# Four-layer graph network: the last 106 attention targets by gathered edge slots instead of in the dense units

## The chip, the cores and the metric

The kernel runs on one core of a Trainium2 chip. The metric is the device time of one execution in microseconds (us). One core has five engines that run their own instruction queues: TensorE (PE; its weight loads are listed as PEld), VectorE (DVE), ScalarE (ACT), GpSimd (POOL) and SyncE (SP). In this kernel SP issues nearly all plain transfers, and POOL issues the indirect ones (gathers).

## The reference

A graph with N = 6250 nodes and E = 206250 directed edges (sorted by target; each node has an edge to itself) passes through four layers. Each one adds its result to x and normalises the row. D = 128, four attention heads of 32 columns.

```python
x = ln(x + L0(x))    # mean over neighbours, two linear maps
x = ln(x + L1(x))    # per edge: relu([x[src], edge_attr] @ W1 + b1) @ W2, mean over a target's edges, then an MLP
x = ln(x + L2(x))    # per target: sum of x[src] and edge_attr through linear maps, then a small MLP
x = ln(x + L3(x))    # graph attention:
    h = (x @ W).reshape(N, 4, 32)
    a_src, a_dst = sum(h * att_src), sum(h * att_dst)          # per node and head
    logits = leaky_relu(a_src[src] + a_dst[dst], 0.2)           # per edge; the kernel's self edge is apart
    alpha = softmax of logits over the edges of a target
    out = segment_sum(h[src] * alpha, dst)
    out = relu(ln(out + bias) * gamma + beta)
```

## The kernel before

The nodes are 49 blocks of 128 (the last has 106). They are tiled as `groups` of four blocks (twelve full groups and one of 106 rows) and as `duos` of two. The fast path, `fast()`, runs four stages one after the other. The order within a stage is written out by hand: generators (`yield` between steps) are advanced a step at a time between the matmuls, and every engine takes its instructions in program order.

**First adjacency product (`dense0`, up to about 840 us).** For each pair of blocks `search` and `find` locate a target's edges by gathers, `sort` holds 64 edge slots per target and marks which are its own (`mine`), and a dense count matrix `A` is built from one-hots by PE and stored in DRAM as `adj` (one row of 256 targets for each pair). The same stage multiplies it with x for layer 0. The lists of all edges (`src_i`, and `dst_r` relative to a chunk's first target `w0b`) are loaded as a whole.

**Edge MLP (`mlp`, to about 3392 us).** The edges run in 147 chunks of 128 x 11. Each chunk is three loads of four or fewer columns; `load` runs five such units ahead and gathers rows of `t1` by `src_i`. `onehot(c)` makes on VectorE the matrix that sums a chunk's edges into a window of 64 targets.

**Second adjacency product (`dense2`).** For each pair of blocks, `load(sb)` brings five tiles of `adj` by SP (four of 704 KB with six buffers, and a smaller one), and 147 matmuls follow. `node2` for the pair before is advanced between them, a step after every ten matmuls; its last step computes the attention logits `al` with VectorE (L523, L525).

**Attention (`attend`).** For a head h and a target's logit, the exponential of the leaky relu is one of two products of a source factor and a target factor, chosen by a comparison. So the sums over all sources are dense matmuls with `adj`. `tables` prepares the source side for a head (h times `us`, split into three bfloat16 parts: ScalarE casts, POOL subtracts the part, L1198). Then for each unit, two groups of targets, 1024 in all, a loop runs over 25 pairs of source blocks. In each step SP loads `A` three steps ahead; ScalarE makes `r` (L1320, two rows), VectorE makes `B` (L1327) and `C` (L1329), PE does five products for each group into `s` (L1347). Six units cover the twelve full groups. The 106 remaining targets are the `more` of the last unit: they have their own load `Am`, their own two VectorE operations `Bm` (L1333, L1334) and five matmuls `sm` (L1349). In the text units are counted from 1 to 6.

Between the steps three lanes are advanced, each by one step every second time: `sums` (`close` of the last unit: copies of s, products with `fold`, division; and `targets` for the next unit), `news` (`tables` for the next head) and `ends` (`finish3`, the final normalisations of a group, started in head 3 and drained after the last matmul).

Of the kernel before, what the change touches and what calls it, by code (L numbers as in the profile page):

```python
# [9 lines left out]
F32 = mybir.dt.float32  # L10
BF16 = mybir.dt.bfloat16
I32 = mybir.dt.int32
# [56 lines left out]
def kernel(  # L69
# [38 lines left out]
    dram = ctx.enter_context(tc.tile_pool(name="dram", bufs=1, space=bass.MemoryType.DRAM))  # L108
    setup = ctx.enter_context(ExitStack())
# [8 lines left out]
    t3 = dram.tile([N, HW], F32)  # L118
    t3d = dram.tile([N + W, 2 * HEADS], F32)
# [24 lines left out]
    src_i = const.tile([P, NCH, T], I32)  # L144
    dst_r = const.tile([P, NCH, T], F32)
# [128 lines left out]

    def prepare_chunks(prep, pps):

        dst_i = dst_r.bitcast(I32)
        nc.vector.memset(src_i[:, NCH - 1, :], 0)
        nc.vector.memset(dst_i[:, NCH - 1, :], -1)
        for to, of in ((dst_i, dst), (src_i, src)):  # L280
            if NF:
                nc.sync.dma_start(to[:, :NF, :], of[: NF * P * T].rearrange("(c p t) -> p c t", p=P, t=T))
            if tail:
                nc.sync.dma_start(to[:tail, NF, :], of[NF * P * T :].rearrange("(p t) -> p t", t=T))
# [25 lines left out]
        nc.vector.tensor_sub(dst_r, dst_r, w0b.unsqueeze(2).to_broadcast([P, NCH, T]))  # L310
# [183 lines left out]
    def node2(acc, al, pool, pps, n0, rows, nb, G=4, hT=None):  # L494
# [32 lines left out]
        if not keep:  # L527
            nc.vector.tensor_copy(hs[:rows, :nb, D:], al[:rows, 0, b0 : b0 + nb, :])
            store(t3, hs, n0, rows, nb)
# [103 lines left out]
    def general():  # L633
        with ExitStack() as st:
            gp = st.enter_context(tc.tile_pool(name="gacc", bufs=1))
            acc = gp.tile([P, 3, NA], F32, name="gacc")
            for k in range(3):
# [4 lines left out]
                           allow_small_or_imprecise_dtypes=True)  # L642
            row_i = gp.tile([P, NCH], I32, name="row_i")
# [3 lines left out]
            def edges(name, rows_of):  # L647
                with tc.tile_pool(name=f"{name}s", bufs=1) as ep, \
# [5 lines left out]
                    nc.vector.tensor_copy(node, dst_r[:, ds(c, 1), :].rearrange("p c t -> p (c t)"))  # L654
                    w0 = ep.tile([P, 1], F32, name="w0")
                    nc.vector.tensor_copy(w0, w0b[:, ds(c, 1)])
                    ri = ep.tile([P, 1], I32, name="ri")
                    nc.vector.tensor_copy(ri, row_i[:, ds(c, 1)])
                    nc.vector.tensor_scalar(node, node, w0, None, op0=ALU.add)
# [96 lines left out]
    def fast():  # L756
# [24 lines left out]

        def onehot(ep, c, bufs=2):
            K = sizes[c]
            oh = ep.tile([P, T, W], F32, name="oh", bufs=bufs)
            nc.vector.tensor_tensor(
                oh[:K], iota[:K, :W].unsqueeze(1).to_broadcast([K, T, W]),
                dst_r[:K, c, :].unsqueeze(2).to_broadcast([K, T, W]), ALU.is_equal)
# [12 lines left out]
        def dense0(stack):  # L800
# [21 lines left out]
            with tc.tile_pool(name="d0o", bufs=1) as one, tc.tile_pool(name="d0", bufs=1) as ep, \  # L822
# [39 lines left out]
                def sort(sb):  # L862
# [5 lines left out]
                    nc.vector.tensor_reduce(degc[:, 2 * sb : 2 * sb + 2], mine, AX.X, ALU.add)  # L868
# [548 lines left out]
```

## Time and profile before

| | |
|---|---|
| Time, median of 5 runs | 5435.55 us (5431.06 to 5441.93) |
| The profiled execution | 5444.59 us, its span 5442.8 us |
| PE busy | 4956.3 us, 91% of the span |
| VectorE, ScalarE, POOL busy | 3008.6, 2594.2, 1989.8 us |
| Mean granted TensorE clock | 0.944 |
| Chain that ended last, by engine | PE 41%, ACT 7%, DVE 5% |

The profile lists groups of instructions by line (L1347 is line 1347 of the kernel before), engine and operation, with `out<-in` by the program's names, the number of instructions, their busy time and the mean of one in ns, then the idle time ahead of them and what ended it. The view in order of time gives start, length and instruction, and in brackets the idle time before it. "SPq" is a transfer being issued by SP. A PE matmul's end is modelled, so busy PE time isn't the same as PE at its peak; a matmul of f32 data shows as two records.

### The profile page before, as it was taken

How to read it: one execution, taken by the hardware profiler on the slowest of the kernel's cores; microseconds unless marked ns; L12 is line 12 of the kernel's file. 1: busy time of each engine (PE TensorE's matmuls, PEld its weight loads, DVE VectorE, ACT ScalarE, POOL GpSimd, SP SyncE). 2: the span in 40 equal slices, each digit the busy share in tenths (PEclk: the TensorE clock that was granted, in tenths of full speed). 3: DMA queues.
4: the chain of work that ended last, by engine and by line, in shares of the span. 5: the costliest groups of instructions: out<-in, count | busy, mean ns of one | idle time of the engine just before them, and what ended most of it. 6: DMA issues, size and time to landing. Idle time of an engine off the chain costs nothing.

```text
span 5442.8 us, 90752 instructions
## 1 busy us (share of the span) xinstructions
PE 4956.3 (91%) x33855; PEld 4079.6 (75%) x33855; DVE 3008.6 (55%) x5084; ACT 2594.2 (48%) x3617; POOL 1989.8 (37%) x1966
## 2 busy tenths in 40 slices
PE   4999998899998998999998998999699999999995
PEld 3999997888888888888888888899455555555553
DVE  6888873233333333333332333222588888888998
ACT  3444442233332333333332332100599999999984
POOL 3334325666666566666666665000110010010000
PEclk9999998898998989999998998999899999999997
DMA  6333334444444444444444443555377777777773
GB/s 120 123 125 141 129 123 134 125 124 128 129 128 124 122 126 128 125 132 126 128 128 125 124 130 117 175 190 190 114 216 219 221 216 228 213 214 228 213 212 118
DMA packets 599589, 834.35 MB, mean 153 GB/s; under 512 B 119837, under 2 KB 484313, under 8 KB 594917
## 3 DMA queue, kind: packets, MB, share of 16 engines
q1 hardware_dynamic: 513077, 603.59, 36.0%
q0 software_dynamic: 85072, 224.21, 14.0%
q8 instruction: 272, 4.46, 0.3%
q14 instruction: 176, 1.44, 0.1%
q10 hardware_dynamic: 992, 0.66, 0.0%
HBM read 738.23 MB, written 89.88 MB: 152 GB/s over the span
## 4 chain that ended last, share of the span: by engine, by line
PE 41%; ACT 7%; DVE 5%; issue 2%; DMA 1%; another core or an unknown queue 1%; POOL 1%; SPq 0%; DVEq 0%; ACTq 0%; POOLq 0%
PE s L1347 13%; PE seg L1107 9%; PE sum L798 7%; PE pre L1093 6%; ACT r L1320 6%; DVE B L1327 2%; PE tp L1082 2%; PE na L1239 1%; DMA A<-adj 1%; PE na L448 0%; SPq L1283 0%; PE sm L1349 0%; DVE sT L1232 0%; ACT acc L1196 0%
## 5 line engine op out<-in xcount | busy, mean ns | idle before, releaser
L127 POOL DMA_INDIRECT g<-t,src_i x1617 | 1571.0, 972 | 962.3 <-issue 756.8
L1320 ACT ACTIVATE r<-ad,bias 128x1024 bf16<-128x1024 f32 (+1 forms) x1176 | 1276.6, 1154 | 90.9 <-DVE B L1327 57.0
L1095 DVE TENSOR_TENSOR g<-g,pre 128x512 f32<-128x512 f32 x882 | 548.7, 640 | 1272.9 <-PE pre L1093 374.0
L1347 PEld LDWEIGHTS <-acc 128*99 128x99 bf16 x5856 | 697.4, 126 | 604.5 <-issue 155.2
L1107 PE MATMUL seg<-oh,g 128*128 128x64 f32 (+1 forms) x6468 | 1026.9, 282 | 51.9 <-issue 47.8
L1107 PEld LDWEIGHTS seg<-oh,g 128*128 128x128 f32 (+1 forms) x6468 | 949.0, 203 | 94.7 <-issue 62.6
L1093 PE MATMUL pre<-W1s,eaT 128*128 128x256 f32 (+1 forms) x3234 | 883.4, 415 | 106.8 <-issue 50.0
L1347 PE MATMUL s<-B,acc 128*99 128x512 bf16 x3504 | 884.2, 382 | 89.5 <-DVE B L1327 84.0
L1096 ACT ACTIVATE g<-g 128x512 f32<-128x512 f32 x882 | 506.7, 592 | 677.6 <-DVE g L1095 440.9
L1093 PEld LDWEIGHTS pre<-W1s,eaT 128*128 128x128 f32 (+1 forms) x3234 | 632.5, 208 | 222.5 <-issue 101.9
L1327 DVE TENSOR_TENSOR B<-A,r 128x2048 bf16<-128x2048 bf16 x600 | 722.8, 1205 | 118.9 <-ACT r L1320 91.8
L1084 ACT COPY eaT<-tp 128x512 f32<-128x512 f32 (+1 forms) x441 | 240.8, 546 | 1055.8 <-remote 312.9
L1107 PE MATMUL seg<-oh,ea 128*128 128x64 f32 (+1 forms) x3234 | 659.1, 285 | 34.0 <-issue 33.2
L1107 PEld LDWEIGHTS seg<-oh,ea 128*128 128x128 f32 (+1 forms) x3234 | 522.6, 202 | 33.7 <-issue 33.3
L907 ACT CAST A<-pa 128x784 bf16<-128x784 f32 x400 | 324.4, 811 | 350.0 <-PE pa L904 322.1
L798 PE MATMUL sum<-A,xs 128*128 128x256 bf16 (+1 forms) x3675 | 469.4, 274 | 0.4 <-ACT A L907 0.4
L1198 POOL TENSOR_TENSOR xs<-xs,acc 128x264 f32<-128x264 f32 (+1 forms) x104 | 103.6, 1004 | 992.9 <-ACT acc L1196 971.4
L1329 DVE TENSOR_TENSOR C<-A,B 128x1024 bf16<-128x1024 bf16 x600 | 430.3, 717 | 63.6 <-PE s L1347 0.8
L798 PE MATMUL sum<-A,acc 128*128 128x256 bf16 (+1 forms) x3675 | 409.3, 271 | 3.3 <-DMA A<-adj 3.3
L798 PEld LDWEIGHTS <-acc 128*128 128x128 bf16 x3675 | 355.1, 98 | 44.8 <-issue 4.8
L798 PEld LDWEIGHTS <-xs 128*128 128x128 bf16 x3675 | 358.4, 102 | 36.2 <-issue 0.6
L904 PE MATMUL pa<-oh,oh 128*128 128x98 bf16 x3200 | 355.9, 269 | 27.6 <-ACT A L907 23.0
(229 smaller groups left out, 4475.6 us busy)
## 6 DMA issues: line engine op xcount, KB each, us to landing
A<-adj SPq DMA_DIRECT2D x2304, 128.0 KB
ea<-in_edge_attr_dram SPq DMA_DIRECT2D x292, 256.0 KB
A<-adj SPq DMA_DIRECT2D x100, 704.0 KB
ea<-in_edge_attr_dram SPq DMA_DIRECT2D x146, 192.0 KB
g<-t,src_i POOLq DMA_INDIRECT x1617
Am<-adj SPq DMA_DIRECT2D x96, 128.0 KB
A<-adj SPq DMA_DIRECT2D x25, 320.0 KB
t<-y SPq DMA_DIRECT2D x24, 256.0 KB
```

Of the source, the lines that this page charges most:

```text
L127: nc.gpsimd.indirect_dma_start(out=to, out_offset=None, in_=table, in_offset=bass.IndirectOffsetOnAxis(ap=index[:K, t : t + 1], axis=0))
L798: nc.tensor.matmul(ps[:, :n], parts[part][:, b, :], a(b)[:, :n], start=k == 0, stop=k == 3 * NB - 1)
L904: nc.tensor.matmul(ps[:, o, q * LO : (q + 1) * LO], ohs[g][0][:, 2 * j + o, :, q], ohs[g][1][:, 2 * j + o, :, q], start=True, stop=True)
L907: nc.scalar.copy(A[sb][:, :, q0 : q0 + 2 * QI].rearrange("p k (o q) -> p k o q", q=QI), ps[:, :, : QI * LO].rearrange("p o (q k) -> p k o ...
L1093: nc.tensor.matmul(pre[:K, t, :], eaT[i][:, b + t, :K], W1s[:, 1, :], start=True, stop=True)
L1095: nc.vector.tensor_add(gb, gb, pre[:K, :n, :])
L1096: nc.scalar.activation(gb, gb, AF.Relu)
L1107: nc.tensor.matmul(ps[:, m, :], rows, oh[c][:K, a + t, :], start=a + t == 0 and m == 0, stop=a + t == T - 1, skip_group_check=True)
L1320: nc.scalar.activation(r[:, l, : n + m], ad[:, : n + m], AF.Relu, bias=bias[:, b + l, h : h + 1], scale=BIG)
L1327: nc.vector.tensor_tensor(wide(bt), At[:, :ns, :kk, :w], wide(r), ALU.min)
L1329: nc.vector.tensor_sub(ct[:, :n].rearrange("p (s q) -> p s q", q=w), At[:, :ns, 0, :w], bt[:, 0, :n].rearrange("p (s q) -> p s q", q=w))
L1347: nc.tensor.matmul(s[to][g][:M, : c1 - c0], row, rhs(c0, c1), start=to not in begun, stop=stop)
```

## The change

The dense units now cover the twelve full groups alone. The 106 targets of the last block are computed from their edge slots: `sort` stores for them the sources (`slot_src`, zero where a slot isn't theirs) and a mask (`slot_not`) in DRAM; `node2` stores h and the source logit of every node in `t3`, a row of 132 numbers; in `attend` a fourth lane, `others`, advances `gathered` every third step. It gathers eight slots at a time, 64 in all, forms the exponentials with VectorE and ScalarE, multiplies and sums with the identity as the stationary operand; the target's own edge comes in as a first matmul. The division and `finish3` follow at once.

To make room in SBUF, the whole edge lists go: `mlp` loads the edges of a chunk from DRAM, six chunks ahead, and `onehot` subtracts `w0b` itself. In `tables`, VectorE subtracts in place of POOL. The tile `s` of `attend` shares the buffer of `neg`.

```diff
@@ storage
+    UNITS = max(1, (len(groups) - 1) // 2)
+    rest = groups[2 * UNITS :]
+    R0 = rest[0][0] // P if rest else NB
+    slot_src = dram.tile([max(2, 2 * NS - R0 // 2 * 2), P, S], I32)
+    slot_not = dram.tile([max(2, 2 * NS - R0 // 2 * 2), P, S], F32)
-    src_i = const.tile([P, NCH, T], I32)
-    dst_r = const.tile([P, NCH, T], F32)
@@ node2
-        if not keep:
+        if keep:
+            for c, of in ((slice(0, D), hs), (slice(D, HW), al[:, 0, b0 : b0 + nb, :])):
+                nc.sync.dma_start(t3[n0 : n0 + n, c].rearrange("(b p) d -> p b d", p=rows), of[:rows, :nb])
+        else:
@@ fast: edges of a chunk
+        def load_edges(c):
+            if c < NCH:
+                edges[c] = edge_pool.tile([P, 2, T], I32, name="edges", bufs=8)
+                for k, of in enumerate((src, dst)):
+                    nc.sync.dma_start(edges[c][: sizes[c], k, :],
+                                      of[c * P * T : c * P * T + sizes[c] * T].rearrange("(p t) -> p t", t=T))
         def onehot(ep, c, bufs=2):
             K = sizes[c]
+            at = ep.tile([P, T], F32, name="at", bufs=2)
+            nc.vector.tensor_scalar(at[:K], edges.pop(c)[:K, 1, :], w0b[:K, c : c + 1], None, op0=ALU.subtract)
...
-                dst_r[:K, c, :].unsqueeze(2).to_broadcast([K, T, W]), ALU.is_equal)
+                at[:K].unsqueeze(2).to_broadcast([K, T, W]), ALU.is_equal)
@@ dense0, sort
+                    if 2 * sb + 2 > R0:
+                        k0 = 2 * sb - R0 // 2 * 2
+                        of = ep.tile([P, 2, S], I32, name="of")
+                        nc.vector.tensor_tensor(of, s, mine, ALU.mult)
+                        nc.sync.dma_start(slot_src[k0 : k0 + 2].rearrange("b p s -> p b s"), of)
+                        none = ep.tile([P, 2, S], F32, name="none")
+                        nc.vector.tensor_scalar(none, mine, -1.0, 1.0, op0=ALU.mult, op1=ALU.add)
+                        nc.sync.dma_start(slot_not[k0 : k0 + 2].rearrange("b p s -> p b s"), none)
@@ dense0, third step
                             flush_dma(nc.sync)
+                            for c in range(6):
+                                load_edges(c)
@@ mlp, load
+                    if a == 0:
+                        load_edges(c + 6)
                     for t in range(k):
-                        gather(g[i][:K, t, :], t1, src_i[:, c, :], a + t, K)
+                        gather(g[i][:K, t, :], t1, edges[c][:, 0, :], a + t, K)
@@ attend
-            units = [(g[0][0], g, []) for g in (groups[k : k + 2] for k in range(0, len(groups), 2))]
-            if len(units) > 1 and len(units[-1][1]) == 1 and units[-1][1][0][2] == 1:
-                units[-2][2].extend(units.pop()[1])
+            units = [(groups[2 * k][0], groups[2 * k : 2 * k + 2]) for k in range(UNITS)]
...
-                s = one.tile([P, NB, HEADS], F32, name="s")
+                s = one.tile([P, NB, HEADS], F32, name="neg")
...
+                shift = one.tile([P, max(1, NB - R0), HEADS], F32, name="shift")
+                es = one.tile([P, max(1, NB - R0), HEADS], F32, name="es")
+                if rest:
+                    nc.vector.scalar_tensor_tensor(shift, s[:, R0:], SLOPE, s[:, R0:], op0=ALU.mult, op1=ALU.max)
+                    nc.vector.tensor_add(es, al[:, 0, R0:], al[:, 1, R0:])
+                    nc.vector.scalar_tensor_tensor(es, es, SLOPE, es, op0=ALU.mult, op1=ALU.max)
+                    nc.vector.tensor_sub(es, es, shift)
+                    nc.scalar.activation(es, es, AF.Exp)
@@ attend, tables
-                                nc.gpsimd.tensor_sub(xs[:, :nb], xs[:, :nb], tab[:, bs, :, k, :])
+                                nc.vector.tensor_sub(xs[:, :nb], xs[:, :nb], tab[:, bs, :, k, :])
@@ attend, the new lane
+                def gathered():
+                    Q = 8
+                    chunks = [(g, j, q) for g, (n0, rows, nb) in enumerate(rest) for j in range(nb) for q in range(0, S, Q)]
+                    def issue(i):
...
+                            rows_of[i] = ep.tile([P, Q, HW], F32, name="g3", bufs=4)
+                            for t in range(Q):
+                                gather(rows_of[i][:, t, :], t3, slots[g, j][0], q + t, P)
+                    for i in range(3):
+                        issue(i)
+                    yield 8
+                    for i, (g, j, q) in enumerate(chunks):
+                        issue(i + 3)
...
+                        if q == 0:
...
+                            nc.tensor.matmul(ps, ident, own, start=True, stop=False)
+                            yield
+                        nc.vector.tensor_add(e, e, al[:, 1, b].unsqueeze(1).to_broadcast([P, Q, HEADS]))
+                        nc.vector.scalar_tensor_tensor(e, e, SLOPE, e, op0=ALU.mult, op1=ALU.max)
+                        nc.vector.tensor_sub(e, e, less[:, q : q + Q])
+                        yield
+                        nc.scalar.activation(e, e, AF.Exp)
+                        yield
+                        xh = x[:, :, :D].rearrange("p t (h c) -> p t h c", h=HEADS)
+                        nc.vector.tensor_mul(xh, xh, e.unsqueeze(3).to_broadcast([P, Q, HEADS, CH]))
+                        yield
+                        for t in range(Q):
+                            nc.tensor.matmul(ps, ident, x[:, t, :], start=False, stop=q + t == S - 1)
+                        yield
+                        if q + Q == S:
...
+                            if j == nb - 1:
+                                ends.add(finish3(go, pool, n0, rows, nb))
+                            yield
@@ attend, main loop
-                sums, news, ends = Lane(), Lane(), Lane()
+                sums, news, ends, others = Lane(), Lane(), Lane(), Lane(3)
+                others.add(gathered())
...
-                            nc.scalar.activation(r[:, l, : n + m], ad[:, : n + m], AF.Relu,
-                                                 bias=bias[:, b + l, h : h + 1], scale=BIG)
+                            nc.scalar.activation(r[:, l, :n], ad[:, :n], AF.Relu, bias=bias[:, b + l, h : h + 1], scale=BIG)
-                        if more:
-                            bm = ep.tile([P, 3, P], BF16, name="Bm")
-                            nc.vector.tensor_tensor(bm[:, :kk, :m], Am[:, :kk, :m], r[:, :kk, n : n + m], ALU.min)
-                            nc.vector.tensor_sub(bm[:, 2, :m], Am[:, 0, :m], bm[:, 0, :m])
...
-                            if more:
-                                nc.tensor.matmul(sm[:M, to, :m], row, rest(), start=not begun, stop=stop,
-                                                 skip_group_check=True)
-                        for lane in (sums, news, ends):
+                        for lane in (sums, news, ends, others):
                             lane.step(now)
```

## The prediction

> **What bounds the kernel now.** I read the busy time in stretches first, one stretch to each stage: the edge MLP (840 to 3392 us), the second adjacency product, its set-up for attention included (to 3858), the attention loop (to 5379) and the tail after its last matmul. Columns are start:end, length, then busy time (instructions) of PE, PEld, DVE, ACT, POOL, the granted PE clock, the DMA share and GB/s.
>
> ```profile
> 840.00:3392.00 2552.00, 2314.89 (x15199) 2105.50 (x15200) 875.84 (x1497) 785.88 (x1419) 1571.53 (x1619) 0.91 0.43 125
> 3392.00:3858.00 466.00, 441.99 (x4009) 393.25 (x4007) 114.25 (x376) 54.80 (x136) 23.52 (x37) 0.97 0.54 178
> 3858.00:5379.00 1521.00, 1434.72 (x7281) 867.39 (x7282) 1330.30 (x1998) 1360.93 (x1442) 98.54 (x96) 0.99 0.71 212
> 5379.00:5443.00 64.00, 4.93 (x36) 4.49 (x36) 45.21 (x177) 7.48 (x20) 0.00 (x0) 0.54 0.08 23
> ```
>
> PE is busy in 94% of the attention loop, with VectorE at 87% and ScalarE at 89% close behind; the tail has no PE work and is VectorE's alone. The same view cut at single units (25 block pairs against two groups of targets) shows what the 106 extra targets cost now. The rows are unit 5 of head 0, unit 6 with the extra targets, units 5 and 6 of head 3:
>
> ```profile
> 4126.80:4186.80 60.00, 58.16 (x285) 34.99 (x284) 52.56 (x70) 56.16 (x64) 6.11 (x6) 1.00 0.71 215
> 4186.80:4254.30 67.50, 65.62 (x407) 41.05 (x406) 60.54 (x111) 59.54 (x56) 1.20 (x1) 1.00 0.80 241
> ...
> 5240.30:5302.80 62.50, 57.43 (x283) 34.81 (x283) 58.94 (x98) 54.25 (x59) 0.00 (x0) 1.00 0.70 213
> 5302.80:5378.90 76.10, 67.60 (x403) 41.36 (x401) 70.46 (x155) 58.06 (x55) 0.00 (x0) 0.98 0.68 203
> ```
>
> Units of heads 0 to 2 run at PE's pace (97%); those of head 3, which also carry the final normalisations, at VectorE's (94%). Then the groups, for the operations that go or are copied (busy, mean ns; then idle before):
>
> ```profile
> L1349 PE MATMUL sm<-Bm,acc 128*99 128x106 bf16 x392 | 82.4, 210 | 6.1 <-DVE Bm L1333 6.1
> L1333 DVE TENSOR_TENSOR Bm<-Am,r 128x212 bf16<-128x212 bf16 (+1 forms) x100 | 26.2, 262 | 0.0
> L1334 DVE TENSOR_TENSOR Bm<-Am,Bm 128x106 bf16<-128x106 bf16 x100 | 21.6, 216 | 3.4
> L1198 POOL TENSOR_TENSOR xs<-xs,acc 128x264 f32<-128x264 f32 (+1 forms) x104 | 103.6, 1004 | 992.9 <-ACT acc L1196 971.4
> ```
>
> **1. The extra targets leave the units.** Unit 6 is 67.5 against 60.0 us, 7.5 more, in heads 0, 1 and 2 alike: 22.5. In head 3 the last unit takes 76.1 against 62.5; about 1 us of that is that its row runs to the last matmul and not to the next unit's start. That leaves 12.6, more because there VectorE sets the pace and Bm's two operations cost 25 x 0.48 = 12 us. Gain **-35** (-32 to -37). ScalarE's shorter r and the missing Am transfers are inside these differences.
>
> **2. The tail gets shorter.** After the last matmul the normalisations queue on VectorE. The end of that queue, in order of time:
>
> ```profile
> 5431.35 1.11 DVE L363 TENSOR_SCALAR xn<-res,mv,rs 128x128 f32<-128x128 f32 x4
> 5432.38 0.28 DVE L618 TENSOR_TENSOR o<-acc,gbc 106x128 f32<-106x128 f32 x1
> ...
> 5436.60 0.35 DVE L363 TENSOR_SCALAR xn<-res,mv,rs 106x128 f32<-106x128 f32 x1
> ```
>
> The 106 rows end at 5436.95, the full group before them at 5432.46: 4.5 us, which move into head 0. Closing their sums (5384.41 to 5386.26) goes too, 1.85. The last store is then the larger one, about +0.3. Together **-6** (-5 to -6.5).
>
> **3. Gathered sums in head 0.** PE: 65 f32 matmuls of 132 columns. An f32 matmul leaves two records; eight of 128 columns take 2.00 us (W4's, L462), 0.25 each, so 65 x 0.25 = 16. The lane steps every third block pair: eight before the first chunk, then some 102 more, so it ends in unit 5 of head 0. The first chunk falls into unit 1, which takes 87 us because PE waits for tables, and is free; seven chunks, 14 us, lie in units where PE is the bound. VectorE: per chunk three small operations at 0.17 (like L1247's reciprocal, 177 ns) and one product of 128x1024 f32 (L439's row has a median of 1224 ns): 1.7 us, eight times 14, with `less`, `own` and the division 15. Two chunks to a unit bring VectorE from 52.6 to about 57 of 63 us, no fuller than in head 3, hence +1. ScalarE: eight small exponentials, nothing. POOL: 64 gathers at 0.97 plus 0.3 of issue, 80 us, under no other POOL work; they are asked for three chunks ahead (36 pairs, 80 us), so a landing of several us is hidden; without that cover, eight landings of about 4 us, +32. Sum **+15** (+8 to +30).
>
> **4. Table differences on VectorE.** POOL took 1004 ns. On VectorE the nearest row is the product of 128x256 f32 from the same tile (L1191, 402 ns): 104 x 0.43 = 45 us. POOL's version also slowed VectorE: C takes 692 ns by the median but 717 in the mean, 25 x 600 = 15 us, and B some 4, so VectorE gains 26 busy us net, 20 of them outside the first unit. How much becomes time? From unit 5 of head 0 to that of head 3, VectorE's 6.4 us more made 2.5 more, 0.4 to one, and that from a higher load; I take +2 (0 to +12). In the first unit POOL's step is on the way: casts follow each other every 0.62 us though one lasts 0.42. Six bursts of such casts can gain up to 1 each. Against it, the tile `s` now waits for the exponentials of `neg`, and `es` puts five operations ahead of the tables, together about +1.2. Net -2 (-5 to +2). Part 4: **0** (-5 to +14).
>
> **5. Edges by chunk.** The MLP gains 294 small transfers on SP (0.33 us each to issue, some 17 us between chunks) and 147 VectorE operations of 128x11, about 0.17 us each, 25 us in all, under VectorE's idle two thirds. What is queued behind `at` is the one-hot and the additions that free PE's `pre`. The one-hot (0.88 us) now makes PE wait 8.5 us in total, so the fifth as much added should give **+2** (0 to +15). Edges are loaded six chunks ahead of the gathers; that cover is about 100 us.
>
> **6. Stores to t3.** In the second product each pair of blocks now ends with two SP stores, and the next pair's A tiles are queued behind them. Today SP asks for such a tile 22 us before its first use (3596.08, use at 3618.3). From now on it must wait for the attention logits:
>
> ```profile
> 3612.95 0.42 DVE L525 TENSOR_REDUCE al<-pr 128x8 f32<-128x256 f32 x1
> ...
> 3618.49 0.47 ACT L1044 ACTIVATE hT<-sum,c1c 128x256 f32<-128x256 f32 x1 [6.94 <-PE sum L798]
> ```
>
> The logits are done at 3613.37, the second store's issue takes 0.37 (as `store` does now), so the tile is asked for at 3613.8 and wanted at 3618.3: 4.5 us. The stage's very first tile shows the price without any cover:
>
> ```profile
> 3391.82 3.66 SPq L1027 DMA_DIRECT2D A<-adj  x7
> ...
> 3396.09 2.29 PE L798 MATMUL sum<-A,acc 128*128 128x256 bf16 x10 [3.30 <-DMA A<-adj]
> ```
>
> 4.27 us. So 22 us of slack become 0.2, and the small packets of the stores stand in front. The thin slack holds for the 17 pairs from the ninth on; before that two steps are taken at a time and the store comes earlier. I take 0.2 us each, **+3** (0 to +20). The Trainium skill, "DMA: Bandwidth & Descriptors", Specifications, speaks against this part: below 512 B a transfer is done as read-modify-write, and the logits go in pieces of 16 B. No row of this trace prices that. As an estimate from that page's 2 us for HBM latency at high load (section Latency and other measured facts), each pair would stall about 2 us, 34 us in all, and the sum would be +10.
>
> Work in the first adjacency product (two VectorE operations and two stores for the last pair, no bulk load of src) lies under a PE that is busy without a gap there: 0, and at most +2 bare.
>
> Sum: -35 - 6 + 15 + 0 + 2 + 3 = **-21**. The profiled execution took 5444.59 us (span 5442.8), so 5423.6; the median of the runs shown is 9.0 lower, and 5435.55 - 21 = **5414**.
>
> **Rivals.** *VectorE becomes the bound in heads 0 to 2.* For it: 87% busy, and head 3 shows what happens at 94%. Against it: the low slope above. If each busy us counted, part 3 gets +13 and part 4 +17 more: -21 + 30 = +9, 5444, within the uncertainty. *SP's stores stall the second product.* A new wait in place of a removed load, at the first tile of 17 pairs. For it: 0.2 us of slack. Against it: without small packets the slack is not negative. At a stall of 2.5 us it costs 17 x 2.5 = 43 in place of 3, net +19, 5454; it makes the change slower by over 0.2% from (21 + 3 + 11)/17 = 2.1 us. *The small edge work shows in the MLP.* If each of 147 chunks loses 0.17 us, +25 for +2: net +2, 5437.
>
> **How the numbers follow.** This kernel's measurement tells about 0.2% (11 us) from no change. Forecast 0.58, VectorE the bound 0.15, SP's stalls 0.15, edges 0.12. Some of the forecast's own range (parts at their high ends) falls within 0.2%, and a few of the rivals' milder forms still come out faster: faster 0.60, same 0.22, slower 0.18. The range goes from the parts' good ends, -37 - 6.5 + 8 - 5 = -40.5, to +15, a stall of 2.3 us: 5395 to 5451.
>
> **What would show it.** Right: unit 6 as long as unit 5 in every head (60 and 62.5); units 2 to 5 of head 0 at 63 to 64; a tail of 58; the second product at its old length within 5 us, PE there waiting for A under 0.5 us at a pair's first tile. Wrong: idle PE before `sum` put down to A; units of heads 1 and 2 over 62; PE waiting for the gathers' chunk; the MLP longer by over 10 us.

## The result, and the profile after

Measured: 5455.97 us (median, 5430.78 to 5476.81) against 5444.18 us for the kernel before, a ratio of 1.0019 with a 95% interval from 1.0011 to 1.0027. So no change by the 0.2% bound, leaning to slower; the prediction was 5414, faster, with a range of 5395 to 5451.

The profiled execution of the changed kernel took 5436.02 us (span 5434.2), 8.6 us *less* than that of before (5444.59). It is a low run of its kernel, 20 us under the median, while the one of before sits on its median. So the profiles say where time moved; that the runs are slower by 12 us they don't say. I come back to this at the end of the experiments.

The stretches by stage, as before the MLP, the second product with the set-up, the attention loop, the tail (start:end, length, busy us and instructions of PE, PEld, DVE, ACT, POOL, granted PE clock, DMA share, GB/s):

```profile
841.00:3390.00 2549.00, 2318.15 (x15196) 2100.53 (x15196) 906.89 (x1642) 784.12 (x1419) 1593.59 (x1617) 0.91 0.44 126
3390.00:3857.00 467.00, 441.40 (x4013) 392.92 (x4011) 119.22 (x389) 56.13 (x139) 24.02 (x35) 0.97 0.51 185
3857.00:5376.00 1519.00, 1423.10 (x6908) 859.71 (x6908) 1313.62 (x1928) 1339.35 (x1444) 66.38 (x59) 0.99 0.70 207
5376.00:5434.00 58.00, 3.88 (x32) 3.55 (x31) 41.02 (x160) 6.29 (x16) 0.00 (x0) 0.54 0.08 24
```

The tail is shorter, 58.5 for 63.9 us (last matmul to end). The MLP, from the first to the last matmul of its edge sums, is 2520.4 us for 2522.1, and the second product, from there to its own last matmul, 442.9 for 442.4. The attention loop is hardly shorter, 1518.4 for 1519.3, though four pieces of work left it. Single units tell why. Rows: units 2 and 3 of head 0 in the kernel before; then, in the changed kernel, units 2 to 6 of head 0 and units 5 and 6 of head 3.

```profile
3945.40:4006.50 61.10, 59.03 (x291) 35.63 (x290) 53.22 (x71) 56.10 (x63) 7.27 (x6) 1.00 0.71 213
4006.50:4066.60 60.10, 57.93 (x285) 35.01 (x284) 52.50 (x72) 56.22 (x64) 6.61 (x7) 1.00 0.72 217
```

```profile
3948.60:4021.10 72.50, 63.32 (x317) 39.44 (x316) 57.20 (x86) 58.47 (x68) 21.69 (x20) 0.98 0.78 192
4021.10:4098.80 77.70, 66.46 (x316) 40.65 (x316) 56.48 (x83) 56.62 (x64) 8.82 (x9) 0.93 0.73 177
4098.80:4163.20 64.40, 59.96 (x311) 37.99 (x310) 56.71 (x85) 55.70 (x64) 0.00 (x0) 1.00 0.66 200
4163.20:4226.10 62.90, 60.46 (x304) 37.19 (x303) 56.64 (x91) 57.86 (x68) 0.00 (x0) 1.00 0.69 208
4226.10:4286.40 60.30, 58.79 (x289) 35.56 (x288) 50.47 (x63) 55.61 (x57) 0.00 (x0) 1.00 0.72 217
5250.00:5312.20 62.20, 57.16 (x281) 34.63 (x281) 58.94 (x98) 53.97 (x58) 0.00 (x0) 1.00 0.71 212
5312.20:5376.00 63.80, 58.92 (x283) 34.68 (x281) 59.74 (x105) 52.66 (x55) 0.00 (x0) 1.00 0.65 194
```

Unit 6 is as short as its neighbours, as forecast. Units 4 and 5 of head 0 (64.4 and 62.9) are where the forecast put all four, 63 to 64. But units 2 and 3 take 72.5 and 77.7 us, and in them PE is busy for 63 and 66 us only: no engine is full, so something is waited for. GpSimd gathers in these units and in unit 1 (20 and 9 instructions in the POOL column, no more from unit 4 on). The waits of head 0, first in the kernel before, then in the changed one (engine, line, what ended the wait: us in total, times, longest):

```profile
DVE B L1327 <- DMA A<-adj: 1.3, 1, 1.3
```

```profile
DVE B L1429 <- DMA A<-adj: 29.9, 16, 4.7
```

VectorE's B waits for the loads of A, 29.9 us in place of 1.3. One such wait in order of time, in unit 3:

```profile
4030.13 1.23 DVE L1429 TENSOR_TENSOR B<-A,r 128x2048 bf16<-128x2048 bf16 x1 [2.76 <-DMA A<-adj]
...
4033.23 1.06 PE L1444 MATMUL s<-A,acc 128*99 128x512 bf16 x2
...
4036.55 0.59 PE L1444 MATMUL s<-A,acc 128*99 128x512 bf16 x2
```

The wait costs more than itself: PE idles with VectorE, and afterwards a pair of matmuls takes 1.06 us until it is back at 0.59. The granted clock of unit 3 is 0.93, that of unit 4 is 1.00. The Trainium skill ("TensorE: Matmul & The Clock Gate", What's actually happening) has a rule for it: after about 3.4 us of idling the array gets half its clock, until it has been busy as long again. The trace agrees in size (1.06 / 0.59 = 1.8) and in length (half the clock is granted for 3.41 us at a time, twice in unit 3). It doesn't agree in the idle time: PE's gaps there are 2.84 and 2.81 us.

### The profile page after: what moved, and what is told of

Its sections match the earlier page's. It is cut to its first block, busy times and chain, and to the rows that moved or that the text cites. A ratio compares the mean times of both kernels' runs of the same rounds, so it can differ in the third digit from the quotient of the medians.

```text
span 5434.2 us, 90840 instructions
## 1 busy us (share of the span) xinstructions
PE 4945.7 (91%) x33477; PEld 4065.3 (75%) x33477; DVE 3022.6 (56%) x5156; ACT 2570.9 (47%) x3618; POOL 1979.7 (36%) x1926
## 3 DMA queue, kind: packets, MB, share of 16 engines
q14 instruction: 184, 1.51, 0.1%
## 4 chain that ended last, share of the span: by engine, by line
PE 35%; ACT 7%; DVE 5%; DMA 2%; issue 2%; SPq 1%; another core or an unknown queue 0%; DVEq 0%; POOL 0%; ACTq 0%; POOLq 0%
PE s L1444 12%; PE sum L822 7%; PE seg L1143 6%; ACT r L1423 6%; PE pre L1129 4%; DVE B L1429 3%; DMA A<-adj 2%; PE na L1282 2%; PE tp L1118 1%; SPq L1390 1%; DVE sT L1275 0%; ACT acc L1239 0%; DVE C L1431 0%; PE na L456 0%; DVE st L362 0%
## 5 line engine op out<-in xcount | busy, mean ns | idle before, releaser
L135 POOL DMA_INDIRECT g<-t,edges x1617 | 1593.6, 986 | 936.2 <-issue 697.2
L1423 ACT ACTIVATE r<-ad,bias 128x1024 bf16<-128x1024 f32 x1176 | 1253.9, 1139 | 104.1 <-DVE B L1429 102.3
L1444 PEld LDWEIGHTS <-acc 128*99 128x99 bf16 x5856 | 736.3, 126 | 654.2 <-issue 160.1
L1143 PEld LDWEIGHTS seg<-oh,g 128*128 128x128 f32 (+1 forms) x6468 | 949.4, 203 | 89.9 <-issue 60.5
L1444 PE MATMUL s<-B,acc 128*99 128x512 bf16 x3504 | 870.5, 383 | 104.7 <-DVE B L1429 89.7
L1431 DVE TENSOR_TENSOR C<-A,B 128x1024 bf16<-128x1024 bf16 x600 | 415.2, 692 | 65.0 <-PE s L1444 2.8
L1444 PE MATMUL s<-C,acc 128*99 128x512 bf16 x1200 | 360.4, 382 | 0.6 <-issue 0.4
```

Source lines behind the costliest of these rows:

```text
L135: nc.gpsimd.indirect_dma_start(out=to, out_offset=None, in_=table, in_offset=bass.IndirectOffsetOnAxis(ap=index[:K, t : t + 1], axis=0))
L1143: nc.tensor.matmul(ps[:, m, :], rows, oh[c][:K, a + t, :], start=a + t == 0 and m == 0, stop=a + t == T - 1, skip_group_check=True)
L1423: nc.scalar.activation(r[:, l, :n], ad[:, :n], AF.Relu, bias=bias[:, b + l, h : h + 1], scale=BIG)
L1431: nc.vector.tensor_sub(ct[:, :n].rearrange("p (s q) -> p s q", q=w), At[:, :ns, 0, :w], bt[:, 0, :n].rearrange("p (s q) -> p s q", q=w))
L1444: nc.tensor.matmul(s[to][g][:M, : c1 - c0], row, rhs(c0, c1), start=to not in begun, stop=stop)
```

## The experiments

They ran on four chips (numbers 0, 5, 6 and 12), on all of which the kernel before takes 4995 to 4998 us (median) and not 5444. Which chip the first pair ran on is not on record. In the profiles of the changed kernel the difference is in the MLP alone. Ratios are to the kernel before, run in turns with them, with the 95% interval.

**What is slow about the gathers.** An empty slot's source is zero in the changed kernel, so it reads row 0 of `t3`. A node has 33 edges on average (206250 / 6250) for 64 slots, so about half of all reads go to one row, and the last chunks consist of little else. First experiment: the empty slots keep the nodes that they hold; their weight still comes out as nothing, so what is computed stays the same.

```diff
-                        nc.vector.tensor_tensor(of, s, mine, ALU.mult)
+                        nc.vector.tensor_copy(of, s)
```

> One edit to the changed kernel: a slot that isn't the target's own keeps the node that it holds instead of row 0 (its weight is still brought to nothing by the 300 that is taken off). Theory A1 (the empty slots all point at row 0 of t3, and many reads of one row are slow: the gathers' packets took about 260 ns each in the first chunks, where slots are filled, and 600 to 1500 ns in the last ones, which are all row 0; they hold the 16 DMA engines, A comes late, VectorE and TensorE wait): packets of all eight chunks take 200 to 350 ns, units 2 and 3 of head 0 fall from 72.5 and 77.7 us to 63 to 66, the wait of B on A in head 0 from 29.9 us to under 12, and the time falls by 20 to 30 us: 0.997 to 0.998 of before. Theory A2 (any gather of 1024 rows does it, or late chunks are slow because they start while A is being loaded): packets stay at 600 ns or more in the late chunks, head 0 as it was, 1.002 of before within 0.001.

Measured 4966.15 us, 0.9942 (0.9928 to 0.9955), while the unedited changed kernel, in turns with it, was at 0.9985. Units 2 to 4 of head 0:

```profile
3495.80:3560.50 64.70, 61.25 (x317) 38.57 (x315) 56.93 (x86) 56.35 (x65) 19.20 (x18) 1.00 0.75 217
3560.50:3626.80 66.30, 61.83 (x318) 38.83 (x317) 56.46 (x84) 57.38 (x66) 12.12 (x10) 1.00 0.72 208
3626.80:3692.80 66.00, 61.83 (x313) 38.73 (x311) 56.83 (x84) 56.02 (x64) 0.00 (x0) 0.97 0.66 193
```

With as many gathers, issued by the same instructions, units 2 and 3 take 64.7 and 66.3 us in place of 72.5 and 77.7. The wait on A:

```profile
DVE B L1429 <- DMA A<-adj: 8.2, 6, 2.4
```

Theory A1 stands: the packets of all eight chunks have a median of 210 to 340 ns, and the run is 22 us under the unedited one. Its ratio of 0.997 to 0.998 was too high, since it took the changed kernel to be at 1.002. What the gathers take of the DMA engines is in the view of the queues (queue, packets, MB, share of 16 engines' time). One chunk in unit 2, first in the changed kernel (17 us), then with the edit (16 us); q0 carries the gathers:

```profile
q0 software_dynamic: 243, 0.54, 40.4%
```

```profile
q0 software_dynamic: 256, 0.54, 17.8%
```

The same 0.54 MB hold the engines for more than twice the time. The run was made again later, beside other kernels:

> The changed kernel with the empty slots left at the node they hold, once more, beside the others of this call. Theory A1 (its gain over the changed kernel is in head 0 of attention alone, which no clock holds down): 18 to 22 us under the changed kernel on any chip, so 0.9942 of before within 0.001 where the MLP is granted 0.99 of the clock, and 0.998 within 0.001 where it is granted 0.91 as in the first profiles. Theory A2 (chance of one chip): back at the changed kernel's ratio.

0.9940 (0.9926 to 0.9953), 4964.29 us, as A1 has it. This version beats both kernels in the later runs. The long MLP of the first pair did not come back, so the 0.998 there is not measured.

**More of it.** All slots point to row 0.

```diff
-                        nc.vector.tensor_tensor(of, s, mine, ALU.mult)
+                        nc.vector.tensor_scalar(of, s, 0.0, None, op0=ALU.mult)
```

> The changed kernel with every slot of the 106 targets, filled ones too, pointing at row 0 of t3: the sums over their neighbours are left out, all else is the same work. Theory A1 (reads of one row by many are what is slow): the gathers' packets take 600 to 1500 ns in all eight chunks in place of the last four alone; units 1 and 2 of head 0, which hold the first five chunks, take 15 to 40 us more than in the changed kernel (92.6 and 72.5 us there), and units 3 and 4 are as there: 1.002 to 1.006 of before on a chip with 0.99 of the clock, where the changed kernel is 0.9985. Theory A2 (it is where and when the gathers run): as the changed kernel, within 0.001.

1.0044 (1.0030 to 1.0058), 5018.40 us. Units 1 and 2 took 112.6 and 78.2 us, 20 and 6 more than in the changed kernel, 26 in all, inside A1's 15 to 40. Units 3 and 4, which A1 left as they were, took 81.0 and 66.0, 2 or 3 us more. The wait on A doubled, and in the 42 us of the first burst of gathers q0 had three quarters of all DMA engines' time:

```profile
DVE B L1429 <- DMA A<-adj: 59.0, 17, 10.9
```

```profile
q0 software_dynamic: 706, 1.51, 74.7%
```

In the version with distinct nodes the first burst (38 us) moved more and held the engines for less than a third of that share:

```profile
q0 software_dynamic: 834, 1.76, 22.3%
```

So the time follows the number of reads of row 0: none 0.994, about half 0.9985, all 1.0044.

**Which sameness.** Two ways of spreading the empty slots, by partition and by slot. In both diffs `part` is 1 where a slot is empty; `nodes_of[:, 0:1]` is the partition's number and `iota` the slot's. "..." stands for lines left out.

```diff
                         nc.vector.tensor_tensor(of, s, mine, ALU.mult)
...
+                        nc.vector.tensor_tensor(part, part, nodes_of[:, 0:1].unsqueeze(2).to_broadcast([P, 2, S]), ALU.mult)
+                        nc.vector.tensor_tensor(of, of, part, ALU.add)
```

> The changed kernel with each empty slot pointing at the row of t3 that has its partition's number, in place of row 0: the 128 rows of one gather are then 128 different ones, while the same 128 rows are read again and again by the later gathers. Theory B1 (what is slow is that many descriptors of one gather read one row at the same moment): packets of the last four chunks at 200 to 400 ns, units 2 and 3 of head 0 at 63 to 67 us, as with the nodes that the slots hold: 0.993 to 0.995 of before where the MLP is granted 0.99 of the clock, about 0.998 where 0.91. Theory B2 (a small region read over and over is slow, whoever reads it): packets at 600 ns or more, units 2 and 3 as in the changed kernel, its ratio.

```diff
                         nc.vector.tensor_tensor(of, s, mine, ALU.mult)
...
+                            nc.vector.tensor_tensor(part[:, k], part[:, k], iota[:, :S], ALU.mult)
+                        nc.vector.tensor_tensor(of, of, part, ALU.add)
```

> The changed kernel with each empty slot pointing at the row of t3 that has the slot's number, in place of row 0: all partitions without a node in that slot still read one row in one gather, but another row than in the gather before. Theory B1 (many descriptors of one gather on one row are slow): packets of the last four chunks at 600 to 1500 ns and units 2 and 3 of head 0 at 70 to 78 us, as in the changed kernel, the same ratio within 0.001. Theory B2 (it is the one row 0 over the whole stretch): packets at 200 to 400 ns, units 2 and 3 at 63 to 67 us, 0.993 to 0.995.

By partition: 0.9942 (0.9929 to 0.9956), the median packet of the last four chunks took 160 to 270 ns; B2, the small region, falls. By slot: 0.9949 (0.9935 to 0.9962), and here B1 falls in the form that I gave it. A gather whose empty partitions all read one row is nearly harmless as long as the next gather reads another row: units 1 to 4 took 90.7, 66.0, 67.0 and 66.0 us, 4 us in all above the version with distinct nodes, though in one stretch of 6 us the median packet still took 880 ns. What hurts is one row over many gathers in a row. A reading that fits all four runs: one row is delivered at a limited rate, and a queue builds up only if gather after gather asks for the same one (the rate is worked out in the last section). That it is a rate is argued; that it needs the same row over gathers is shown.

**What the gathered sums cost without that.** The version with distinct nodes, with its 64 gathers replaced by one GpSimd `memset` per chunk, so that the 106 targets get no neighbours; all other work on the chunks stays.

```diff
-                            for t in range(Q):
-                                gather(rows_of[i][:, t, :], t3, slots[g, j][0], q + t, P)
+                            nc.gpsimd.memset(rows_of[i], 0.0)
```

> The changed kernel with empty slots left at the node they hold, and its 64 gathers in attention left out: each tile of eight slots is set to zero by one GpSimd instruction instead, so the 106 targets get no neighbours; all work of VectorE, ScalarE and TensorE on the tiles stays. With gathers, units 2 to 5 of head 0 took 64.7, 66.3, 66.0 and 63.0 us against 59.9 to 60.2 without the gathered sums. Theory C1 (what is left of the cost is TensorE's 65 sums with the identity and the work around them, as the prediction summed it): these units stay at 63 to 66 us, 0.993 to 0.995 of before where the MLP is granted 0.99 of the clock. Theory C2 (it is the transfers of the gathers, which still take DMA engines from A): they fall to 60 to 62 us, 12 to 16 us less in all, 0.991 to 0.992.

0.9946 (0.9932 to 0.9959), no faster than with gathers. Units 2 and 3:

```profile
3488.50:3552.00 63.50, 61.26 (x316) 38.75 (x316) 56.77 (x86) 55.55 (x62) 1.95 (x2) 1.00 0.68 201
3552.00:3617.40 65.40, 61.60 (x318) 38.76 (x317) 56.54 (x84) 57.20 (x66) 0.98 (x1) 1.00 0.67 196
```

C1 stands. Here are head 0's six units side by side (us), and in the last column units 1 to 5 summed against the first row. The first row has attention as in the kernel before.

| | 1 | 2 | 3 | 4 | 5 | 6 | units 1 to 5 |
|---|---|---|---|---|---|---|---|
| edges by chunk alone (attention of before) | 87.6 | 59.9 | 60.2 | 60.2 | 60.0 | 67.7 | 0 |
| table differences by VectorE alone (next paragraph) | 82.0 | 61.9 | 60.2 | 60.4 | 59.9 | 67.3 | -4 |
| gathered sums, no gathers | 87.0 | 63.5 | 65.4 | 65.4 | 63.0 | 60.3 | +16 |
| gathers of distinct nodes | 88.6 | 64.7 | 66.3 | 66.0 | 63.0 | 58.7 | +21 |
| changed kernel (last run) | 88.1 | 75.5 | 78.1 | 64.3 | 63.0 | 58.7 | +41 |
| all slots on row 0 | 112.6 | 78.2 | 81.0 | 66.0 | 62.9 | 58.7 | +73 |

PE's sums and what is around them are 16 us more than the first row, the transfers of spread gathers 4 or 5 more, row 0 another 20. The changed kernel has the table differences on VectorE too, which alone shorten these units by 4, so the sums and what is around them cost some 20, 5 of them in unit 1.

**The other parts alone, on the kernel before.** The table differences by VectorE (L1198, `nc.gpsimd.tensor_sub` to `nc.vector.tensor_sub`, nothing else):

> The kernel before with one line of the change alone: the tables' differences by VectorE in place of GpSimd. Theory A (what the prediction took: 104 differences are hidden in VectorE's idle time): 1.000 within 0.0008, heads 1 to 3 as before within 3 us each. Theory B (VectorE is the bound there): each of the 78 differences of heads 1 to 3 shows in full, +0.2 us each at the least, 15 us and over, 1.003.

0.9987 (0.9978 to 0.9996), 4992.00 us: if anything a gain. Heads 1 to 3 keep their lengths; unit 1 of head 0, where PE waits for tables, took 82.0 us and not 87.6. B falls; A's 1.000 within 0.0008 was a little too high.

The stores of the second product (the hunk of `node2` alone, `if keep:` with two stores to `t3`):

> The kernel before, with one part of the change alone: the second product's nodes are also stored to t3, two DMAs for each group of nodes, one of them 16 B a node. Theory A: nothing, 1.000 within 0.0008, second product 441 to 445 us. Theory B (the narrow stores hold up SP's queue or the DMA engines): +8 to +20 us, 1.0015 to 1.004, and the second product longer by that.

1.0011 (1.0002 to 1.0020), 4999.86 us; second product 444.6 us in the profile, 442.3 to 443.5 in those of the edges alone. So a few us rather than none: A's 1.000 within 0.0008 was too narrow, B's 8 us and more too much.

The edges by chunk (the hunks of `load_edges`, `onehot`, `prepare_chunks` and `load` alone), three times:

> The kernel before, with one part of the change alone: the edges' sources and targets are loaded by chunk in the MLP, through the ring of eight, with the subtraction of the window's start per chunk. Theory A (the loss is all in head 0): no change that a timing can tell, 1.000 within 0.0008, MLP 2520 to 2526 us. Theory B (the small loads before each chunk and the added VectorE instruction cost time in the MLP): +8 to +20 us, 1.0015 to 1.004 of before, and the MLP's length in the profile above that of before at an equal granted clock.

> The kernel before with the edges loaded by chunk in the MLP and nothing else, once more. The first time the chip granted 0.99 of the clock in the MLP, which took 2063 us there, and the edit made no difference (0.9995, from 0.9986 to 1.0004). The first pair of profiles had 0.91 granted in the MLP and 2520 us. Theory A (the edges by chunk cost nothing at any clock): 1.000 within 0.001. Theory B (they cost time only where the clock is held down in the MLP, which would make up the difference between 1.0019 there and 0.9985 here): where the granted clock of the MLP is near 0.91 again, 1.003 to 1.005, some +20 us; where it is 0.99, 1.000 again, and this run tells nothing on it.

> The kernel before with the edges loaded by chunk in the MLP alone, a third time. In the first pair of profiles the MLP is full of stretches in which TensorE issues one matmul in over 1 us with nothing to wait for, each followed by half the clock (447 us of half clock before, 420 after); the later runs have 14 to 21 us of it. Theory A (the part of the changed kernel in the MLP lengthens these stretches): 1.003 to 1.005 of before if this run has them, as then the changed kernel's 1.0019 would come from here. Theory B (it does nothing to them): 0.998 to 1.000 with them or without. If this run has none, it only narrows what the part costs without them: 0.999 within 0.001.

0.9995 (0.9986 to 1.0004), 0.9987 (0.9978 to 0.9996) and 0.9991 (0.9981 to 1.0000): no cost where the MLP is short. With the long MLP of the first pair it was not tried.

**The changed kernel again, and the long MLP.**

> The changed kernel once more, unedited, for a second profile of it. The pair of profiles so far has the changed kernel 8.6 us ahead while the median of its timed runs lies about 12 us behind that of before. Theory A (the lost time is in head 0, where transfers of A come late behind the gathers, and varies there): the six units of head 0 again take some 430 us against 396 in before, within 15 us, and what makes this run longer or shorter than the 5436.0 us of the first profile shows in head 0. Theory B (the lost time is in the MLP, where the small loads of edges stand in SP's queue): head 0 takes the same 430 us within 5, and the MLP is 2530 us or more in place of 2520.4. Theory C (the profile was merely a fast one, the clock that the throttle granted in the MLP sets the spread): MLP up with a granted clock under 0.913, everything else as in the first profile. Timed: 1.002 of before within 0.001.

> The changed kernel, unedited, a third time. Theory A (its ratio hangs on how far the clock is held down in the MLP): 0.9985 of before within 0.001 where the MLP is granted 0.99 of the clock, 1.002 where it is 0.91. Theory B (0.9985 was chance): 1.001 to 1.003 whatever the clock.

> The changed kernel, unedited, a fourth time, beside the run with the edges by chunk alone. If the MLP has the stretches of half clock of the first pair: 1.002 of before, and the stages of the profile say whether the MLP is longer than 2522 us or head 0 longer than 430. If not: 0.999 within 0.001, head 0 at 428 to 432 us.

0.9985 (0.9976 to 0.9994), 0.9990 (0.9981 to 0.9999), 0.9982 (0.9973 to 0.9991): 6 to 10 us *faster* than before, the opposite sign of the first pair's 1.0019; the 1.002 expected of the second run rested on the long MLP. In that run's profile every stage but one has within 2.1 us the length that it had in the first: first product 837.7 (838.8 there), second 445.0 (442.9), attention loop 1518.3 (1518.4), tail 58.5 (58.5). The MLP takes 2071.5 and not 2520.4. The granted clock by slices of the span, first in the changed kernel's first profile, then in that of its second run:

```profile
PEclk9999998899998998998999998999899999999998
```

```profile
PEclk9999998999999999999999999998999999999997
```

What PE waits for in the MLP, in the first profile (three rows), and in the last run (the only row):

```profile
PE seg L1143 <- issue: 74.3, 136, 1.7
PE pre L1129 <- DVE g L1131: 50.0, 58, 3.4
PE pre L1129 <- issue: 36.4, 61, 2.3
```

```profile
PE pre L1129 <- DVE g L1131: 7.1, 11, 3.2
```

In the first pair PE stands still with nothing to wait for that the profile shows. The clearest such stretch:

```profile
1012.52 0.26 PE L1143 MATMUL seg<-oh,g 128*128 128x64 f32 x1 [1.48 <-issue]
1013.95 0.27 PE L1143 MATMUL seg<-oh,g 128*128 128x64 f32 x1 [1.16 <-issue]
1015.34 0.27 PE L1143 MATMUL seg<-oh,ea 128*128 128x64 f32 x1 [1.12 <-issue]
1016.74 0.26 PE L1143 MATMUL seg<-oh,ea 128*128 128x64 f32 x1 [1.14 <-issue]
```

One record per 1.4 us, while otherwise they follow each other at 0.11. Three or more such gaps in a row are rare (four times in this profile); mostly it is one or two. In the MLP of either kernel the granted clock falls to half some 60 times in the first pair, for 440 us in the profile of before and 421 in that of the changed kernel, against 5 to 33 us in the later runs. Together they make up most of the difference: PE's waits in the first profile's MLP add up to some 207 us, and 421 us at half the clock cost, by my estimate, up to 210. The kernel before has both too, so the change doesn't make them. The times also spread more: the changed kernel's runs lie within 46 us in the first pair and within 8 in its first eleven later ones. The loads of instructions are as many and as large in both (124 in the MLP, 2.03 MB, 0.3% or 0.4% of the DMA engines' time), so they don't tell the two apart.

What stays open: in the first pair's profiles the stages outside the MLP are 7 us shorter in the changed kernel (8.6 less the MLP's 1.7), and the runs 12 us longer. Some 20 us should then lie in the MLP, the one stage whose length moves so much; no profile shows them there. Whether the edges by chunk lengthen the stretches there, or something else does, no run here shows.

## Why the prediction was wrong

In the profiles, every part but one came inside its range or a few us better.

- *Part 1, the units without the extra targets, -35.* Unit 6 went from 67.5, 67.4 and 67.3 to 60.3, 58.8 and 58.7 us, and in head 3 from 73.4 to 61.0 (from its first B to its last): -37. Right.
- *Part 2, the tail, -6.* 63.9 to 58.5: -5.4. The chain of the full group's normalisation now ends it:

```profile
5425.33 0.87 DVE L362 BATCH_NORM_STATS2 st<-res 128x6 f32<-128x128 f32 x4
...
5427.06 1.11 DVE L371 TENSOR_SCALAR xn<-res,mv,rs 128x128 f32<-128x128 f32 x4
5428.19 0.37 SPq L132 DMA_DIRECT2D out_dram<-xn  x1
```

- *Part 3, gathered sums, +15 (+8 to +30).* **This is the step that failed.** In the first pair of profiles units 1 to 5 of head 0 took 5.4, 11.4, 17.6, 4.1 and 2.9 us more: +41, outside even its own range. PE's sums were sized well, 16.5 us measured for 16. The run without gathers is 20 us above the table differences alone, so the work around the sums was put some 4 us low; the first chunk, called free in unit 1, costs 5 there together with the operations on `es`. The larger miss is another: what failed is the sentence on the cover, "a landing of several us is hidden; without that cover, eight landings of about 4 us". Nothing in PE's or VectorE's queue waits for a landing, so it was indeed hidden. But the sum asked only who waits for the gathers, and not whom they keep waiting: A's loads use the same 16 engines, with a DMA share of 0.70 already, and come three steps of 2.4 us ahead. Spread gathers cost 4 or 5 us in this way, and those of row 0 another 20. That half of the indices would be zero stands in the diff (`of` is `s` times `mine`) and in the sizes (33 edges, 64 slots); I read both and put no price on it.
- *Part 4, table differences, 0 (-5 to +14).* VectorE's version takes what was said, 427 ns against the 430 summed (first row; the second is part 3's sums with the identity, 16.5 us where 16 was said):

```profile
L1241 DVE TENSOR_TENSOR xs<-xs,acc 128x264 f32<-128x264 f32 x88 | 37.3, 427 | 1.5 <-ACT acc L1239 0.5 <-issue 0.3
L1348 PE MATMUL sg<-g,ident 128*128 128x132 f32 x128 | 16.5, 284 | 0.0
```

  Alone the part gave 0.9987, at the good end of the range, from unit 1 of head 0. The rival that made VectorE the bound falls: heads 1 and 2 keep 57.7 to 60.5 us a unit.
- *Part 5, edges, +2 (0 to +15).* `at` takes 235 ns, not the 170 assumed, 34.6 us in all, all of it hidden: the MLP of the profile is 1.7 us shorter, and alone the part is at 0.999. What it does in the runs with the long MLP stays open.
- *Part 6, stores to t3, +3 (0 to +20).* 442.9 for 442.4 us in the first pair; alone 1.0011, some 5 us (1 to 10). The slack is a little more than was worked out: the tile is asked for at 3612.07 and first used at 3617.4, 5.3 us where 4.5 was said. The logits' store is issued behind its reduction, the next A tile directly behind that:

```profile
3611.61 0.37 SPq L537 DMA_DIRECT2D t<-al  x1
...
3612.07 2.89 SPq L1061 DMA_DIRECT2D A<-adj  x5
...
3617.61 0.47 ACT L1078 ACTIVATE hT<-sum,c1c 128x256 f32<-128x256 f32 x1 [6.94 <-PE sum L822]
```

  and PE's wait for A in the whole second product is 4.6 us, 1.3 more than before:

```profile
PE sum L822 <- DMA A<-adj: 4.6, 2, 3.3
```

  That 1.3 us is one wait at the fifth pair's first tile, where under 0.5 was said; the 17 pairs from the ninth on don't wait. The rival of SP's stalls (17 pairs at 2.5 us) falls. The estimate of 34 us made from the Trainium skill's page "DMA: Bandwidth & Descriptors" (Specifications, pieces under 512 B, and Latency and other measured facts) is not what the runs show: the part with its 16 B pieces costs about 5 us in all, by the timed runs.

With +41 in place of +15 the sum is +5; the profiles' -8.6 is lower since parts 1 and 4 to 6 came out some 13 us better than put down (the largest piece is part 4's, units 1 to 5 of heads 1 to 3 being 5.5 us shorter in all). The signs named beforehand read the same way: unit 6, the tail and the second product as said, units 2 and 3 of head 0 at 72.5 and 77.7 where 63 to 64 was said. So the 42 us between the forecast of 5414 and the 5456 measured have three sources. The profiles came out 12 us above their forecast: the missed 26 us of part 3, less the 13 gained elsewhere. The base moved by 9: I started from 5435.55, the median of five runs, and 77 runs of the kernel before have 5444.18. The last 20 lie between the changed kernel's profile and its runs, and no step of mine covered them, since I took the MLP to be of one length from run to run. Without the long MLP the change gains 6 to 10 us, still less than half of what was forecast.

## What to carry to other kernels

Where an index list is padded, pad it with spread rows (the partition's number will do) and not with zero: here that one line is worth some 22 us, as much as the whole forecast gain. A new transfer that nobody waits for still has a price, which is read at the loads that it runs beside: their DMA share and how far ahead they are asked for. And a difference of 0.2% between two profiled executions is worth no more than the spread of the runs they are drawn from, so compare the stages that the change doesn't touch first.

## What the runs showed of the hardware

Reads of one row of 528 B by many gathers were slow: in the burst with all slots on row 0, q0 moved 1.51 MB in 42 us, which is about 68 rows per us or 15 ns for each. Distinct rows went at 1.76 MB in 38 us, 88 rows per us, near the pace at which GpSimd issued them (128 rows per 1.25 to 1.4 us). Meanwhile the gathers' packets held the DMA engines longer (a median of 1200 to 1500 ns for a packet of eight rows, against 160 to 380), and the queue of A's loads, q1, had 20.6% of their time in that burst, against 45.1% in the burst with distinct rows.

The same program took some 450 us more in the MLP in the first pair than in all later runs on four chips, with nearly equal lengths of all other stages. The extra time is in short gaps between matmul records (90 of 1.0 to 1.7 us in the changed kernel's profile, and a few longer) and in some 60 periods of half the granted clock. The Trainium skill ("TensorE: Matmul & The Clock Gate", What's actually happening and, for the peak-current limiter, Seeing it yourself) knows half the clock, as the state after idling, and a state of 13/16; the records here have 1.0 and 0.5 only, and no run shows what starts the gaps.
